# Attention of the first batch: when denominators, their inverses, the bias of v and the weight sums are done

## The chip, the cores and the metric

The kernel runs on one core of a Trainium2 chip. The metric is the device time of one execution in microseconds. The median of three runs of the kernel before is 2653.88 us (2652.91 to 2655.13).

## What is computed

Two layers on x of shape (4, 1024, 32, 32), everything in float32. Only the first one matters here; the second (three convolutions with batch norms and a residual) follows it and is not touched. Cut to what matters, for each of the four batches and N = 1024 tokens:

```python
x = hidden_states.reshape(B, C, N).transpose(0, 2, 1)
qkv = (x @ w_qkv.T + b_qkv).reshape(B, N, 3, nh, hd)      # 16 heads of 64
q, k = rmsnorm(rope(q)), rmsnorm(rope(k))
attn = softmax(einsum("bqhd,bkhd->bhqk", q, k) * hd ** -0.5)
ctx = einsum("bhqk,bkhd->bqhd", attn, v)
out = rmsnorm(ctx @ w_proj.T) + x
```

The kernel divides by the softmax's denominator after the product with v: the context of a head, summed over unnormalised exponentials, is multiplied by the inverse of the sum of the exponentials, and the bias of v is added at the end.

## The kernel before

**Stages.** The batches go one after the other through four projections (q, k, v, and the output projection after attention) and an attention. The projections are done by a fast matrix multiplication (Strassen's in Winograd's form, two levels), which needs sums of weight blocks. These sums are the same for every batch, so they are made once, during batch 0, and kept in DRAM (`wd`, `wd2`). A good part of them is made during batch 0's attention: 21 "parts" (the list `todo` in `program`, four from `prepare_blocks` and seventeen from `prepare`). A part loads four tiles of 128x512 through the SP queue into four buffers of a ring of eight (`chunk`), VectorE does four additions on them (lines 409 to 412 or 392 to 395), and the POOL queue writes the four results to DRAM (lines 414 or 397). At most two parts are loaded and waiting (`made`); `load_parts` fills up to two at score tile 3 of each unit.

**The attention's loop.** `attention` (line 767) handles one half of the queries (512 of 1024, `c` is 0 or 1), and in it eight pairs of heads (`hp`). One pair of heads in one half is called a unit here; batch 0 has sixteen, numbered 0 to 15. In a unit there are eight tiles of keys (`t`). For each, TensorE makes a score tile in PSUM (line 781, three buffers "sc", each of two banks), ScalarE its exponential (line 788) and VectorE adds it to the pair's running sum `d_` (lines 799 and 801). Then TensorE makes the contexts of the pair from the eight exponentials (line 810, one buffer "cx"), and ScalarE copies them out (lines 816, 819).

**Denominators.** Every second unit completes two pairs of heads. `late` holds their step: `sums_of_four` (line 856) sums the two `d_` over the partitions by eight matmuls with ones (line 863) into a buffer of the pool of the score tiles; `inverses` (line 905) copies that to SBUF by ScalarE (line 910) and sends it through DRAM, by the SP queue, into a tile of 128x16 (`to_few`, lines 898 and 902), on which the reciprocal is short (line 914); the result goes back to DRAM (line 915) and is spread over 64 partitions for each head (`spread`, line 932, two DMAs on SP). The step in `late` is taken at score tile 1 of the unit after the pair's; the reciprocal and what follows at that unit's end (`half_done`). At the end of the next odd unit `mean_of_v` (line 761) multiplies the contexts by the inverses on VectorE (line 764) and adds the bias of v on POOL (line 765). For the last two pairs `last_inverses` (line 920) is called at the end of the attention: reciprocal on a tile of 128x512 (line 924), DMAs by POOL, and the multiplication three products into the output projection (`means`). A buffer of scores named "skip" is taken before the last denominator.

**Order.** All engines but the queues work in the order in which the program is written (`manual_schedule`). In the projections a hand-written clock counts products: `after(n, step)` puts a step n products later, `product_done` advances the clock. The extra work in the attention (`extra`, the parts) is taken at the end of each unit, as many as a rounded share says (line 842). The batches 1 to 3 have no parts in their attention; in their first half (`fold`) they gather the sums of four pairs in two tiles T0 and T2 and treat them otherwise.

Of the kernel before, what the change touches and what calls it, by code (L numbers as in the profile page):

```python
# [11 lines left out]
F32 = mybir.dt.float32  # L12
AF = mybir.ActivationFunctionType
ALU = mybir.AluOpType
# [4 lines left out]
P = 128  # L19
# [4 lines left out]
NHP = C // (2 * HD)  # L24
CH = 512
NCH = N // CH
# [35 lines left out]
NH = NT // 2  # L62
# [23 lines left out]
def program(ctx, tc, x, wblk, w2, w3, vecs, cos, sin, out, bad):  # L86


    nc = tc.nc
# [26 lines left out]
    def col(name, i=0):  # L116
        return vec[:, COL[name] + i : COL[name] + i + 1]
# [40 lines left out]
    with tc.tile_pool(name=f"st{u}", bufs=2) as st, ExitStack() as s:  # L158

        tp = s.enter_context(tc.tile_pool(name=f"tp{u}", bufs=1))  # L160
# [24 lines left out]
        half = [slice(c * CH, (c + 1) * CH) for c in range(NCH)]  # L185
# [17 lines left out]
        def bank(kind, name):  # L203
            pool, shape = psum[kind]
            return pool.tile(shape, F32, tag=kind, name=name)
# [48 lines left out]
        def after(n, step):  # L254
            later.append((pace["at"] + n, step))
# [505 lines left out]
        def mean_of_v(q_all, c, hp, w, engine=nc.gpsimd):  # L761

            cx = q_all[:, hp, half[c]]
            nc.vector.tensor_tensor(cx, cx, w, ALU.mult)  # L764
            engine.tensor_scalar(cx, cx, col("bv", hp), None, ALU.add)  # L765

        def attention(b, c, q_all, k_all, v, probs_, late, ready, extra, slow, steps_in_all, load_parts, fold, then):


            at = half[c]  # L770
            sums_, contexts = [], []
            for hp in range(NHP):
                n = f"{b}_{c}_{hp}"
                rows = shifts(q_all, k_all, n, hp, c) if bad is None else None
                probs = []
                for t in range(N // P):
                    p = probs_[:, t]
                    sc = bank("sc", f"sc_{n}_{t}")
                    for keys in (low, high):
                        for j, d in enumerate((low, high)):  # L780
                            nc.tensor.matmul(  # L781
                                sc[keys, j], k_all[d, hp, t * P + keys.start : t * P + keys.stop], q_all[d, hp, at],
                                start=True, stop=bad is not None,
                            )
                    if bad is None:
                        for j in range(2):
                            nc.tensor.matmul(sc[:, j], ones[0:1, :], rows[j], start=False, stop=True)
                    nc.scalar.activation(p, sc, AF.Exp)  # L788
                    if t == 1:
                        if late:  # L790
                            late.pop(0)()
                        if fold and hp % 2 == 0:
                            d_ = fold[hp // 4][:, hp % 4 // 2 * 2 : hp % 4 // 2 * 2 + 2, :]
                        else:
                            d_ = acc.tile([P, 2, CH], F32, tag="tot", name=f"den_{n}")
                    if t == 3:
                        load_parts()
                    if t == 1:
                        nc.vector.tensor_tensor(d_, probs[0], p, ALU.add)  # L799
                    elif t > 1:  # L800
                        nc.vector.tensor_tensor(d_, d_, p, ALU.add)  # L801
                    probs.append(p)
                if (c, hp) == (NCH - 1, NHP - 1):
                    then()
                o = bank("cx", f"cx_{n}")
                for t in range(N // P):
                    for j in range(2):
                        h0 = (2 * hp + j) * HD
                        for i, keys in enumerate((low, high)):
                            nc.tensor.matmul(  # L810
                                o[j * HD : (j + 1) * HD, i], v[keys, t, h0 : h0 + HD], probs[t][keys, j],
                                start=(t == 0), stop=(t == N // P - 1),
                            )

                cx = q_all[:, hp, at]
                nc.scalar.copy(cx, o[:, 0])  # L816
                if b == 0 and (c, hp) != (NCH - 1, NHP - 1):
                    other = temp(f"cx_{n}")
                    nc.scalar.copy(other, o[:, 1])
                    nc.gpsimd.dma_start(cx, other, accum_op=ALU.add)  # L820
                else:
                    contexts.append((cx, o[:, 1]))
                sums_.append(d_)
                if hp % 2 == 1:
                    for r in ready:
                        mean_of_v(q_all, *r)
                    ready.clear()
                if fold:
                    halve(hp, d_, fold[hp // 4][:, hp % 4 // 2 * 2 : hp % 4 // 2 * 2 + 2, :])
                    if hp % 4 == 3:  # L830
                        eights.append((hp + 2, lambda n=n, hp=hp: sum_of_eight(b, n, hp, fold[hp // 4], ready)))
                if half_done and half_done[0][0] <= c * NHP + hp:
                    half_done.pop(0)[1]()
                if slow:
                    slow.pop(0)()

                if waiting:
                    next_waiting()
                slots = NCH * NHP - 1
                if extra and steps_in_all == 0 and hp > 0:  # L840
                    extra.pop(0)()
                for _ in range(len(extra) - -(-steps_in_all * max(slots - 1 - c * NHP - hp, 0) // slots) if steps_in_all else 0):
                    extra.pop(0)()
                if contexts:
                    nc.vector.tensor_tensor(contexts[0][0], *contexts.pop(0), ALU.add)
                if eights and eights[0][0] <= c * NHP + hp:
                    eights.pop(0)[1]()
                if hp % 2 == 0 or fold:
                    continue
                if (c, hp) == (NCH - 1, NHP - 1):  # L850
                    last_inverses(b, c, hp, n, sums_of_four(n, sums_), ready)
                else:
                    late.append(lambda n=n, hp=hp, ds=sums_: inverses(b, c, hp, n, sums_of_four(n, ds), ready))
                sums_ = []

        def sums_of_four(n, sums_):
            if n == f"0_{NCH - 1}_{NHP - 1}":
                bank("sc", f"skip_{n}")
            dn = bank("sc", f"dn_{n}")[:, 0]
            for i, d_ in enumerate(sums_):  # L860
                for j in range(2):
                    q = slice((2 * i + j) * QH, (2 * i + j + 1) * QH)
                    nc.tensor.matmul(dn[q, :], ones[:, :QH], d_[:, j], start=True, stop=True)  # L863
            return dn

        half_done, eights = [], []
        low, high = slice(0, P // 2), slice(P // 2, P)

        def halve(hp, d_, home):
# [35 lines left out]
        def inverses(b, c, hp, n, dn, ready):  # L905


            r = temp(f"rec_{n}")
            k = 2 * ((b * NCH + c) * NHP + hp - 1)
            nc.scalar.copy(r, dn)  # L910
            few, rows = to_few(n, k, 4, r[::QH, :])

            def invert():
                nc.vector.reciprocal(few, few)
                nc.sync.dma_start(rows, few)
                spread(c, hp, n, ready, [dens[k + j : k + j + 3 : 2, :] for j in range(2)])

            half_done.append((0, invert))

        def last_inverses(b, c, hp, n, dn, ready):  # L920
            k = 2 * ((b * NCH + c) * NHP + hp - 1)
            r = temp(f"rec_{n}")
            nc.scalar.copy(r, dn)
            nc.vector.reciprocal(r, r)
            nc.gpsimd.dma_start(dens[k : k + 4, :], r[::QH, :])
            spread(c, hp, n, ready, [dens[k + j : k + j + 3 : 2, :] for j in range(2)], nc.gpsimd)
# [263 lines left out]
        for b in range(B):  # L1190
# [29 lines left out]
            v = room  # L1220
# [30 lines left out]
            slow = [lambda: None] * 3 + [lambda f=f: add_residual(f) for f in range(NT)] if b > 0 else []  # L1251
            probs_ = xp.tile([P, N // P, 2, CH], F32, tag="x", name=f"p_{b}")
            fold = [None, None]
            if b > 0:

                fold[0] = [tp.tile([P, NH, CH], F32, tag=t, name=f"den_{b}_{t}") for t in ("T0", "T2")]
# [8 lines left out]
            for c in range(NCH):  # L1265
                if (b, c) == (B - 1, NCH - 1):
                    extra = filters()
                attention(
                    b, c, q_all, k_all, v, probs_, late, ready, extra, slow, steps_in_all, load_parts, fold[c], then
                )  # L1270
            psum_for("proj")
            room = v_room(f"to_{b}")
# [50 lines left out]
        w = conv1_weights("last")  # L1323
# [364 lines left out]
```

## Time and profile before

| | us |
|---|---|
| median of three runs | 2653.88 |
| profiled execution | 2659.62 |
| its span, first to last instruction | 2657.8 |
| TensorE matmul busy | 2628.8 (99%) |
| VectorE busy | 2142.4 (81%) |
| ScalarE busy | 1120.3 (42%) |
| POOL busy | 474.6 (18%) |
| batch 0's attention, first score tile to the projection's first product | 289.61 to 522.41 |
| batch 1's attention, the same | 868.62 to 1095.39 |

A busy TensorE is counted from overlapping matmuls, so the share of 99% hides waits that are shorter than the work around them; these are read from the starts of consecutive groups in the timeline. Lines of the timeline have the start, the duration, the engine, the line of the kernel, the operation, the tiles written and read, the shapes and the count; a bracket holds the idle time before it and what ended it. PEld is the loading of weights into TensorE, SPq and POOLq are queues that issue DMAs.

### The profile page before, as it was taken

The numbers are of one execution on the slowest core, as the hardware profiler recorded it, in microseconds if no ns is written. First come the engines' busy times: TensorE is split into PE (matmuls) and PEld (weight loads), VectorE is DVE, ScalarE is ACT, GpSimd is POOL, SyncE is SP. The second block draws the span as 40 slices with busy tenths as digits, with TensorE's granted clock in tenths as the row PEclk, the third lists the DMA queues.
The fourth block names the chain that finished last, engine by engine and source line by source line (L and its number), as shares of the span: only waits on it lengthen the run. The fifth ranks groups of instructions, "written<-read, shape, count | busy, mean of one in ns | idle before, by whom it ended". The sixth has DMA issues, their size and how long they took to land.

```text
span 2657.8 us, 40523 instructions
## 1 busy us (share of the span) xinstructions
PE 2628.8 (99%) x15434; PEld 1628.7 (61%) x15434; DVE 2142.4 (81%) x2595; ACT 1120.3 (42%) x1568; POOL 474.6 (18%) x592
## 2 busy tenths in 40 slices
PE   9999999999999999999999999999999999999997
PEld 4448533488888333688886333888884335846843
DVE  4577899997787877888888767987988779877987
ACT  2222465523342555433343555233425654312266
POOL 2542243401011221200111222000111221020000
PEclk9999999999999999999999999999999999999999
DMA  7897788777577452467776531666774443683165
GB/s 270 290 263 211 214 245 245 238 223 232 174 189 212 82 103 59 117 186 222 186 190 166 96 77 35 211 204 177 193 212 90 85 105 85 208 278 96 64 238 206
DMA packets 252794, 463.66 MB, mean 174 GB/s; under 512 B 32176, under 2 KB 124896, under 8 KB 252592
## 3 DMA queue, kind: packets, MB, share of 16 engines
q1 hardware_dynamic: 196672, 287.80, 35.2%
q0 software_dynamic: 47856, 156.40, 23.6%
q10 hardware_dynamic: 8064, 16.78, 1.8%
q8 instruction: 125, 2.05, 0.3%
q14 instruction: 77, 0.63, 0.1%
HBM read 329.53 MB, written 97.01 MB: 160 GB/s over the span
## 4 chain that ended last, share of the span: by engine, by line
PE 66%; DVE 1%; DMA 1%; ACT 0%; issue 0%; ACTq 0%
PE sc L781 13%; PE cx L810 12%; PE p_y L485 9%; PE p_v L480 8%; PE p_q L485 6%; PE p_k L485 6%; PE c L1592 4%; PE c2x L1453 2%; PE c L1015 2%; PE c2y L1453 2%; PE c L974 1%; PE c1s L1015 1%; PE dn L863 0%; DVE V L1388 0%; PE c1a L1015 0%; DMA cosT<-in_cos_dram 0%
## 5 line engine op out<-in xcount | busy, mean ns | idle before, releaser
L788 ACT ACTIVATE p<-sc 128x1024 f32<-128x1024 f32 x512 | 478.1, 1049 | 17.7 <-PE sc L781 17.4
L781 PE MATMUL sc<-q,k 64*64 64x512 f32 x4096 | 456.2, 591 | 0.0
L801 DVE TENSOR_TENSOR den<-den,p 128x1024 f32<-128x1024 f32 x312 | 385.2, 1235 | 37.2 <-ACT p L788 5.1
L810 PE MATMUL cx<-p,to 64*64 64x512 f32 x3072 | 338.3, 589 | 0.0
L781 PEld LDWEIGHTS sc<-q,k 64*64 64x64 f32 x4096 | 149.6, 132 | 293.7 <-ACT p L788 149.5
L810 PEld LDWEIGHTS cx<-p,to 64*64 64x64 f32 x3072 | 117.5, 133 | 212.1 <-issue 211.0
L480 PE MATMUL p_v<-w_v,x 128*128 128x256 f32 x928 | 210.1, 380 | 1.0 <-DVE x L451 1.0
L485 PE MATMUL p_y<-q,w_y 128*128 128x256 f32 x928 | 209.8, 380 | 0.7 <-issue 0.7
L485 PEld LDWEIGHTS p_y<-q,w_y 128*128 128x128 f32 x928 | 176.1, 190 | 27.7 <-issue 4.1
L480 PEld LDWEIGHTS p_v<-w_v,x 128*128 128x128 f32 x928 | 176.2, 190 | 26.1 <-DVE x L451 2.0
L816 ACT COPY q<-cx 128x512 f32<-128x512 f32 x64 | 37.5, 585 | 348.1 <-PE cx L810 348.1
L765 POOL TENSOR_SCALAR q<-q,vec 128x512 f32<-128x512 f32 x56 | 111.6, 2002 | 290.0 <-DVE q L764 290.0
L485 PE MATMUL p_q<-to,w_q 128*128 128x256 f32 x672 | 152.2, 380 | 0.0
L485 PE MATMUL p_k<-to,w_k 128*128 128x256 f32 x672 | 152.2, 380 | 0.0
L485 PEld LDWEIGHTS p_q<-to,w_q 128*128 128x128 f32 x672 | 127.7, 190 | 18.5 <-issue 1.2
L485 PEld LDWEIGHTS p_k<-to,w_k 128*128 128x128 f32 x672 | 127.6, 190 | 18.3 <-issue 1.2
L810 PE MATMUL cx<-p,rq 64*64 64x512 f32 x1024 | 112.8, 589 | 0.0
L1592 PE MATMUL c<-h,w 128*128 128x512 f32 x256 | 110.3, 593 | 0.5 <-ACT h L1495 0.5
L799 DVE TENSOR_TENSOR den<-p 128x1024 f32<-128x1024 f32 x52 | 63.5, 1222 | 42.8 <-ACT p L788 42.8
L801 DVE TENSOR_TENSOR den_T<-den_T,p 128x1024 f32<-128x1024 f32 x72 | 88.2, 1225 | 7.9 <-DVE den_T L801 0.5
L480 PE MATMUL p_v<-w_v,t 128*128 128x256 f32 x384 | 90.1, 379 | 1.2 <-DMA w_v<-wdf 1.2
L485 PE MATMUL p_y<-to,w_y 128*128 128x256 f32 x384 | 90.3, 380 | 0.2 <-DMA w_y<-wdf 0.2
(497 smaller groups left out, 4308.8 us busy)
## 6 DMA issues: line engine op xcount, KB each, us to landing
w_v<-wd2f SPq DMA_DIRECT2D x112, 256.0 KB, 2.9
w_y<-wd2f SPq DMA_DIRECT2D x112, 256.0 KB, 3.1
w_q<-wd2f SPq DMA_DIRECT2D x84, 256.0 KB, 3.0
w_k<-wd2f SPq DMA_DIRECT2D x84, 256.0 KB, 2.8
wd2f<-w_pre POOLq DMA_DIRECT2D x68, 256.0 KB, 4.5
q<-qs POOLq DMA_DIRECT2D x64, 256.0 KB, 5.5
k<-ks POOLq DMA_DIRECT2D x64, 256.0 KB, 4.5
x1df<-y POOLq DMA_DIRECT2D x32, 512.0 KB, 6.1
```

Of the source, the lines that this page charges most:

```text
L480: nc.tensor.matmul(o[:, q].rearrange("p (g f) -> p g f", g=2), r[:, i, q * P : (q + 1) * P], wt[:, :, i, :], skip_group_check=True, **at,)
L485: nc.tensor.matmul(o[:, q], wt[:, q, i, :], r[:, i, :], skip_group_check=True, **at)
L765: engine.tensor_scalar(cx, cx, col("bv", hp), None, ALU.add)
L781: nc.tensor.matmul(sc[keys, j], k_all[d, hp, t * P + keys.start : t * P + keys.stop], q_all[d, hp, at], start=True, stop=bad is not None,)
L788: nc.scalar.activation(p, sc, AF.Exp)
L799: nc.vector.tensor_tensor(d_, probs[0], p, ALU.add)
L801: nc.vector.tensor_tensor(d_, d_, p, ALU.add)
L810: nc.tensor.matmul(o[j * HD : (j + 1) * HD, i], v[keys, t, h0 : h0 + HD], probs[t][keys, j], start=(t == 0), stop=(t == N // P - 1),)
L816: nc.scalar.copy(cx, o[:, 0])
L1015: nc.tensor.matmul(o, wt[:, i, :], rows(i), start=first and i == 0, stop=last and i == NH - 1, skip_group_check=True,)
L1453: nc.tensor.matmul(o[:, r * TR * TC : (r + 1) * TR * TC], uw[2 * h + r, j][:, i * PL + f * P : i * PL + (f + 1) * P], vt[b, i][:, 2 * h + ...
L1592: nc.tensor.matmul(os[i], w3t[k][f // NH][:, f % NH, :], h2[b, k][:, half[c]], start=(k == 0), stop=(k == NPT - 1),)
```

## The change

In batch 0 alone (`b == 0`), except for the rounding of the parts, which only batch 0 has:

- The step in `late` (denominators of two pairs) is taken behind score tile 3 instead of tile 1. The running sums are kept in four slots of two tiles, T0 and T2 (`own`), instead of two buffers of the pool `acc`.
- The reciprocal, its DMA back and the spread (`half_done`) are put one unit later: at score tile 2 of the next odd unit, instead of the end of the unit of the denominators.
- At the end of an odd unit VectorE still multiplies by the inverses; the bias of v is now added by ScalarE (`mean_and_bias`, `biases`), behind the exponentials of tiles 5 and 6 of the next unit. In the last unit VectorE does both.
- The last denominators are put half a step of the clock (one block of eight matmul instructions) into the output projection, in a buffer of that stage's pool "o2"; "skip" goes.
- The number of weight parts taken at the end of each unit is rounded the other way. By unit they were 1, 1, 2, 1, 2, 1, 1, 2, 1, 2, 1, 1, 2, 1, 2 and are 2, 1, 2, 1, 1, 2, 1, 2, 1, 1, 2, 1, 2, 1, 1.

```diff
--- before.py
+++ after.py
@@ -764,7 +764,7 @@
             nc.vector.tensor_tensor(cx, cx, w, ALU.mult)
             engine.tensor_scalar(cx, cx, col("bv", hp), None, ALU.add)
 
-        def attention(b, c, q_all, k_all, v, probs_, late, ready, extra, slow, steps_in_all, load_parts, fold, then):
+        def attention(b, c, q_all, k_all, v, probs_, late, ready, extra, slow, steps_in_all, load_parts, fold, then, own):
 
 
             at = half[c]
@@ -786,10 +786,16 @@
                         for j in range(2):
                             nc.tensor.matmul(sc[:, j], ones[0:1, :], rows[j], start=False, stop=True)
                     nc.scalar.activation(p, sc, AF.Exp)
+                    if t == (3 if b == 0 else 1) and late:
+                        late.pop(0)()
+                    if t in (5, 6) and biases:
+                        biases.pop(0)()
+                    if b == 0 and t == 2 and half_done and half_done[0][0] <= c * NHP + hp:
+                        half_done.pop(0)[1]()
                     if t == 1:
-                        if late:
-                            late.pop(0)()
-                        if fold and hp % 2 == 0:
+                        if b == 0:
+                            d_ = own[hp % 4 // 2][:, hp % 2 * 2 : hp % 2 * 2 + 2, :]
+                        elif fold and hp % 2 == 0:
                             d_ = fold[hp // 4][:, hp % 4 // 2 * 2 : hp % 4 // 2 * 2 + 2, :]
                         else:
                             d_ = acc.tile([P, 2, CH], F32, tag="tot", name=f"den_{n}")
@@ -823,7 +829,12 @@
                 sums_.append(d_)
                 if hp % 2 == 1:
                     for r in ready:
-                        mean_of_v(q_all, *r)
+                        if b > 0:
+                            mean_of_v(q_all, *r)
+                        elif (c, hp) == (NCH - 1, NHP - 1):
+                            mean_of_v(q_all, *r, nc.vector)
+                        else:
+                            mean_and_bias(q_all, *r)
                     ready.clear()
                 if fold:
                     halve(hp, d_, fold[hp // 4][:, hp % 4 // 2 * 2 : hp % 4 // 2 * 2 + 2, :])
@@ -839,7 +850,7 @@
                 slots = NCH * NHP - 1
                 if extra and steps_in_all == 0 and hp > 0:
                     extra.pop(0)()
-                for _ in range(len(extra) - -(-steps_in_all * max(slots - 1 - c * NHP - hp, 0) // slots) if steps_in_all else 0):
+                for _ in range(len(extra) - steps_in_all * max(slots - 1 - c * NHP - hp, 0) // slots if steps_in_all else 0):
                     extra.pop(0)()
                 if contexts:
                     nc.vector.tensor_tensor(contexts[0][0], *contexts.pop(0), ALU.add)
@@ -848,22 +859,36 @@
                 if hp % 2 == 0 or fold:
                     continue
                 if (c, hp) == (NCH - 1, NHP - 1):
-                    last_inverses(b, c, hp, n, sums_of_four(n, sums_), ready)
+
+                    def last(ds=sums_):
+                        last_inverses(b, c, hp, n, sums_of_four(n, ds), ready)
+
+                    if b == 0:
+                        after(0.5, last)
+                    else:
+                        last()
                 else:
                     late.append(lambda n=n, hp=hp, ds=sums_: inverses(b, c, hp, n, sums_of_four(n, ds), ready))
                 sums_ = []
 
         def sums_of_four(n, sums_):
             if n == f"0_{NCH - 1}_{NHP - 1}":
-                bank("sc", f"skip_{n}")
-            dn = bank("sc", f"dn_{n}")[:, 0]
+                dn = bank("o2", f"dn_{n}")
+            else:
+                dn = bank("sc", f"dn_{n}")[:, 0]
             for i, d_ in enumerate(sums_):
                 for j in range(2):
                     q = slice((2 * i + j) * QH, (2 * i + j + 1) * QH)
                     nc.tensor.matmul(dn[q, :], ones[:, :QH], d_[:, j], start=True, stop=True)
             return dn
 
-        half_done, eights = [], []
+        half_done, eights, biases = [], [], []
+
+        def mean_and_bias(q_all, c, hp, w):
+            cx = q_all[:, hp, half[c]]
+            nc.vector.tensor_tensor(cx, cx, w, ALU.mult)
+            biases.append(lambda: nc.scalar.activation(cx, cx, AF.Identity, bias=col("bv", hp)))
+
         low, high = slice(0, P // 2), slice(P // 2, P)
 
         def halve(hp, d_, home):
@@ -915,7 +940,7 @@
                 nc.sync.dma_start(rows, few)
                 spread(c, hp, n, ready, [dens[k + j : k + j + 3 : 2, :] for j in range(2)])
 
-            half_done.append((0, invert))
+            half_done.append((c * NHP + hp + 2 if b == 0 else 0, invert))
 
         def last_inverses(b, c, hp, n, dn, ready):
             k = 2 * ((b * NCH + c) * NHP + hp - 1)
@@ -1251,6 +1276,9 @@
             slow = [lambda: None] * 3 + [lambda f=f: add_residual(f) for f in range(NT)] if b > 0 else []
             probs_ = xp.tile([P, N // P, 2, CH], F32, tag="x", name=f"p_{b}")
             fold = [None, None]
+            own = None
+            if b == 0:
+                own = [tp.tile([P, NH, CH], F32, tag=t, name=f"den_{b}_{t}") for t in ("T0", "T2")]
             if b > 0:
 
                 fold[0] = [tp.tile([P, NH, CH], F32, tag=t, name=f"den_{b}_{t}") for t in ("T0", "T2")]
@@ -1266,7 +1294,7 @@
                 if (b, c) == (B - 1, NCH - 1):
                     extra = filters()
                 attention(
-                    b, c, q_all, k_all, v, probs_, late, ready, extra, slow, steps_in_all, load_parts, fold[c], then
+                    b, c, q_all, k_all, v, probs_, late, ready, extra, slow, steps_in_all, load_parts, fold[c], then, own
                 )
             psum_for("proj")
             room = v_room(f"to_{b}")
```

## The prediction

> **What bounds the kernel now.** I read the stage table first, then TensorE's timeline, then VectorE's and the queues' in batch 0's attention, which is all that the change touches.
>
> ```profile
> core 0: us, PE busy (x) PEld busy (x) DVE busy (x) ACT busy (x) POOL busy (x), PEclk, DMA share, GB/s
> 283.00:526.00 243.00, 241.91 (x2160) 86.17 (x2160) 222.33 (x236) 142.62 (x172) 92.31 (x124) 1.00 0.78 236
> 857.00:1096.00 239.00, 239.00 (x2154) 88.55 (x2153) 184.10 (x176) 134.98 (x154) 52.44 (x47) 1.00 0.37 75
> ```
>
> TensorE (PE) bounds both stages. But batch 0 (first row) also has VectorE (DVE) at 222 of 243 us and the DMA engines at 0.78, where batch 1 (second row) has 184 of 239 and 0.37: in batch 0 VectorE is nearly a second bound.
>
> ```profile
> 374.52 1.90 PE L781 MATMUL sc<-q,k 64*64 64x512 f32 x16
> 376.35 1.91 PE L863 MATMUL dn<-den,ones 128*32 128x512 f32 x8
> 378.19 5.38 PE L781 MATMUL sc<-q,k 64*64 64x512 f32 x48
> ...
> 463.66 1.06 PE L863 MATMUL dn<-den,ones 128*32 128x512 f32 x8
> 464.65 5.38 PE L781 MATMUL sc<-q,k 64*64 64x512 f32 x48
> ...
> 519.21 1.05 PE L863 MATMUL dn<-den,ones 128*32 128x512 f32 x4
> 520.62 1.05 PE L863 MATMUL dn<-den,ones 128*32 128x512 f32 x4 [0.36 <-DVE den L801]
> 522.41 3.69 PE L485 MATMUL p_y<-q,w_y 128*128 128x256 f32 x16 [0.73 <-issue]
> ```
>
> The only loss is at the denominators. Undisturbed, one costs 0.99 us to the next start (463.66 to 464.65). In unit 6 (a unit is one pair of heads of one half, counted 0 to 15) it costs 1.84, in unit 10 1.56 (434.46 to 436.02), and the last takes 3.20 to the projection's first product. Lost: 0.85 + 0.57 + 2.2 = **3.62 us**. That is what the change can win. The last 0.73 is labelled "issue", but the product starts at 522.38, just after ScalarE's copy of that denominator ends at 522.31 (L923, 521.72 + 0.585): I take it as that wait.
>
> ```profile
> 318.87 0.69 DVE L409 TENSOR_TENSOR w_blk<-w_blk,w_blk 128x512 f32<-128x512 f32 x1
> ...
> 321.65 1.22 DVE L799 TENSOR_TENSOR den<-p 128x1024 f32<-128x1024 f32 x1
> 322.97 7.87 DVE L801 TENSOR_TENSOR den<-den,p 128x1024 f32<-128x1024 f32 x6
> 332.80 0.25 DVE L914 RECIPROCAL few<-few 128x16 f32<-128x16 f32 x1 [1.96 <-DMA few<-densf]
> ```
>
> VectorE's unit is read here: weight sums (four operations, 2.75 us a part), then seven additions (9.11 us to the next start), then the inverse, which waited 1.96 us for its round trip.
>
> ```profile
> L406 SPq DMA_DIRECT2D w_blk<-in_wblk_dram x5: 328/328/328, 318.5 to 327.0; - x5
> DMA to landing us min/median/max: 5.0/5.7/6.0
> ```
>
> The loads of the third weight part start at 318.5, when the first part's writes (issued by POOL from 310.09) have landed and its ring buffers are free; the fourth is issued at 320.4 and lands 6 us later, at **326.5**.
>
> ```profile
> 505.98 0.33 SPq L915 DMA_DIRECT2D densf<-few  x1
> 508.71 1.26 SPq L932 DMA_DIRECT2D inv<-densf  x2
> 511.75 2.08 SPq L383 DMA_DIRECT2D w_y<-in_wblk_dram  x2
> ```
>
> SP's queue runs in order: inverse back, its spread, then the projection's first weights.
>
> [...]beside POOL's bias (L765, 2.0 us each) two of four weight sums per pair take 0.98 to 1.06 us, not 0.69. [...]The 8 KB inverses land 1.4 to 5.2 us after issue: [...]the spread is load. [...]Around each 128*32 denominator among 64*64 tiles the neighbouring groups are some 0.16 us long; the change keeps their number.
>
> **The change, part by part.** TensorE's base: a unit is 13.74 us (6.87 scores + 6.87 contexts), one with a denominator 14.89.
>
> (1) *Denominator behind score tile 3 instead of 1.* It moves 2 x 0.86 us later, to unit start + 3.54; its second half, which needs the newer sum, to + 4.05. Both old stalls inside the stage go if the sum is there by then. The four `own` sums free VectorE of the two-buffer limit. ScalarE's copy moves along, and SP's two DMAs behind it.
>
> (2) *Weight parts sooner.* Parts popped per unit were 1,1,2,1,2,1,1,2,1,2,1,1,2,1,2; now 2,1,2,1,1,2,1,2,1,1,2,1,2,1,1. No work is added, but unit 0 now makes two. Follow VectorE from the first part, 306.98: + 2 x 2.75 + 9.11 = 321.6 for unit 1's sum. Unit 2 starts at 317.13, its denominator wants that sum at 321.2: **0.4 lost**. Next VectorE wants the third part, one unit sooner than before. It lands at 326.5 at the earliest I can argue from its buffers: VectorE idles 4.9 us. Then 326.5 + 2.75 + 9.11 (unit 2) + 2 x 2.75 + 9.36 (unit 3, inverse included) = 353.2. Unit 4 starts at 317.13 + 14.89 + 0.4 + 13.74 = 346.2 and wants the sum at 350.2: **3.0 lost**. Bounds: 0.2, if loads landed in 3.2 us; 4.2, if the second part's writes, now in the same stretch, delay them by 1.2.
>
> (3) *Inverses a unit later* (at tile 2 of the odd unit, behind the first addition). VectorE no longer waits for `few` (4.1 us in three waits). But the multiplication by the spread inverse (L764) keeps its place, so reciprocal, DMA back, spread of two DMAs must now fit beside six additions: 8.1 us. In the trace reciprocal to landed spread takes 8.4, 7.0, 6.9, 10.6, 11.1, 8.9 and 9.4 us: mean 8.9. This is the **added wait**: some 0.7 us per pair, at least 0, at most 3.0. Behind it on VectorE stand the weight sums, the next additions, hence the next denominator. A pair of units costs VectorE 2 x 9.11 + 0.25 + 2 x 0.6 + 3 x 2.75 = 27.9, with the wait 28.6, TensorE 13.74 + 14.89 = 28.6: even. After unit 4 the later sums stand some 2.5 us ahead of their denominators (units 6, 8, 10: for instance 380.3 against 382.8), so I book **0**. SP's loads behind the spread start some 3 us later in odd units; that meets the same slack.
>
> (4) *Bias of v by ScalarE.* Off POOL: 12 x 2.0 us; VectorE wins back 6 x 0.7 us (used above: undisturbed 2.75). On ScalarE: 12 x 0.72 us (the same form, L631, 719 ns), behind tiles 5 and 6. ScalarE is busy 143 of 243 us; exponentials 6 and 7 come at most 1.4 us later, and contexts want tile 6 only 5.2 us after scores end: 0. Without that cover it would be 8.6 us. The two biases of the last pair but one go to VectorE: 2 x 0.55 us, in (5).
>
> (5) *Last denominators in the projection.* They stand behind its first product (1.73 us), in a bank of its own pool; the 2.2 us go if unit 15's sum is ready. By the chain above it ends some 0.5 to 1 us before. But SP reaches the projection's first weights only behind the spread of unit 15, now some 6.5 us later in the unit: issued at about unit start + 9.3, needed at 13.74, and the row above landed 5.7 us after issue, with two parts' writes in the way instead of one: **0.3**, 0 to 1.5. In the projection VectorE does the reciprocal of 3.35 us and sums behind two more operations; the sum wanted by the tenth product was 3.2 us early (534.83 against 538.0) and is now about even: **0.3**, 0 to 1.5.
>
> Sum: -3.62 + 0.4 + 3.0 + 0 + 0.3 + 0.3 = **+0.4 us**. Against the profiled execution's 2659.62 us (span 2657.8) that is 2660.0; the median of the runs, 5.7 us lower, is shifted alike: 2653.88 + 0.4 = 2654.3. Everything after the projection is paced by TensorE's products and moves along.
>
> **Rivals.** *A, the forecast*: the gain is given back at unit 4; 2652.6 to 2656. *B, the gain stays*: the third part lands in some 3.2 us. For it: loads elsewhere take 2.8 us (w_y, minimum). Against: DMA share in this stretch is 0.8. -3.62 + 0.4 + 0.2 = -3.0: 2650.9. *C, slower: VectorE becomes the bound through the wait for the spread.* If it takes 10.8 us, as in two of seven, each pair waits 2.7 and falls 2.0 us behind; four such pairs after unit 4, less 0.8 in the pair with two parts, less the 2.5 ahead: 4.7 us on top of A, 2659.0. It decides from a mean of about 9.5 us on. For it: the reciprocal now stands behind the weight sums, whose writes are then in flight. Against: SP's queue is otherwise empty there. *D*: TensorE's wait at 651 us for `w_q` (2.13 us, and the next eight matmuls took 3.68 instead of 1.89) goes or doubles: 3.9 us either way; nothing in its surroundings changes.
>
> **Numbers.** A 0.48, B 0.27, C 0.21, D 0.04. The range reaches from B's end with all stalls gone and a run's spread of 1 us, 2649.5, to C's 2659.2; less than 2 in 10 is left out. A measurement here tells 0.2% (5.3 us) from no change. Under 2648.6: part of B and D, 0.04; over 2659.2: C's tail and D, 0.09; between, 0.87.
>
> **What would show it.** Right: in the profile after, the denominators of units 6 and 10 cost 1 us, that of unit 4 some 4, VectorE idle near 322 to 326 for a `w_blk` load; 128x512 bias rows on ACT. Wrong: unit 4 without a stall (B), or stalls in units 8 to 14 with VectorE idle for `inv` (C).

## The result and the profile after

The kernel after takes **2683.74 us** (median of five runs, 2680.84 to 2686.30), the kernel before 2653.88 (2652.91 to 2655.73) beside it: ratio 1.0113, 95% interval 1.0101 to 1.0124. It is 30 us slower where 0.4 us was forecast. The profiled execution took 2682.35 us with a span of 2680.5, 22.7 us more than that of before, which lay 5.7 us over the median of its own runs.

The stage of the change can be timed without that spread: from the first score tile of batch 0 to the last product of its projection. Before: 289.61 to 607.25, **317.64 us**. After: 287.90 to 632.55, **344.65 us**, so +27.0. The remaining difference of the spans comes from elsewhere: the stage starts 1.7 us sooner, and between the projection and batch 1's attention 2.7 us less is lost (the wait at 651 us was 2.13 us with slow matmuls behind it, and is 1.28 now).

The stage table of the kernel after, first the stage that the prediction showed, then two stretches in which the granted clock (third number from the end) fell:

```profile
283.00:526.00 243.00, 232.43 (x2032) 78.87 (x2034) 196.98 (x212) 143.88 (x175) 62.88 (x104) 0.99 0.74 219
...
415.30:422.10 6.80, 5.69 (x24) 1.47 (x28) 3.54 (x5) 1.69 (x3) 0.00 (x0) 0.50 0.43 128
541.60:551.80 10.20, 6.33 (x15) 3.82 (x12) 9.83 (x12) 0.58 (x1) 0.58 (x1) 0.50 0.21 54
```

TensorE is busy 232 us of 243 instead of 242, VectorE 197 instead of 222: VectorE has not more to do, it waits. TensorE's timeline of the kernel after (start, duration, line, tiles, count, idle time and what ended it):

```profile
348.70 1.05 PE L882 MATMUL dn<-den_T,ones 128*32 128x512 f32 x4
352.10 1.05 PE L882 MATMUL dn<-den_T,ones 128*32 128x512 f32 x4 [2.35 <-DVE den_T L807]
353.09 3.67 PE L781 MATMUL sc<-q,k 64*64 64x512 f32 x32
...
412.28 1.05 PE L882 MATMUL dn<-den_T,ones 128*32 128x512 f32 x4
416.41 1.92 PE L882 MATMUL dn<-den_T,ones 128*32 128x512 f32 x4 [3.08 <-DVE den_T L807]
418.26 5.54 PE L781 MATMUL sc<-q,k 64*64 64x512 f32 x32
...
536.56 2.00 PE L485 MATMUL p_y<-q,w_y 128*128 128x256 f32 x8
538.49 1.05 PE L882 MATMUL dn<-den_T,ones 128*32 128x512 f32 x4
541.41 1.82 PE L882 MATMUL dn<-den_T,ones 128*32 128x512 f32 x4 [1.87 <-DVE den_T L807]
547.09 3.78 PE L485 MATMUL p_y<-q,w_y 128*128 128x256 f32 x8 [3.87 <-DVE q L856]
```

Wherever TensorE loses time here, a denominator's second half waits for the newer of the two sums (`den_T`, VectorE); at the end the second product waits too, for VectorE's addition of the last contexts (L856). Against the undisturbed 14.89 us, the units 2, 4, ... 14 are longer by 0.98, 3.39, 2.92, 6.87, 0.97, 1.87 and 3.47 us: 20.5, where before lost 1.4 in them. From the start of unit 15 to the projection's end it is 109.84 us instead of 101.89: 7.95 more. 20.5 - 1.4 + 7.95 = 27.0, the whole difference. In unit 8 and at the end the granted clock fell to 0.50 around the wait. In unit 8 the second half of the denominators took 1.85 us to the next start instead of 0.99, and the group of 32 score matmuls behind it 5.37 us (418.26 to 423.63) instead of 3.48: 2.75 of the 6.87 us.

What VectorE waited for between 283 and 551 us (us in all, times, the longest), and its timeline around two of these waits:

```profile
DVE q L889 <- DMA inv<-densf: 21.6, 5, 6.5
DVE w_blk L409 <- DMA w_blk<-in_wblk_dram: 5.4, 1, 5.4
DVE q L889 <- PE sc L781: 4.0, 1, 4.0
```

```profile
325.39 0.69 DVE L409 TENSOR_TENSOR w_blk<-w_blk,w_blk 128x512 f32<-128x512 f32 x1 [5.36 <-DMA w_blk<-in_wblk_dram]
...
407.00 1.22 DVE L805 TENSOR_TENSOR den_T<-p 128x1024 f32<-128x1024 f32 x1
408.38 0.25 DVE L939 RECIPROCAL few<-few 128x16 f32<-128x16 f32 x1 [0.16 <-DMA few<-densf]
408.55 7.81 DVE L807 TENSOR_TENSOR den_T<-den_T,p 128x1024 f32<-128x1024 f32 x6
419.59 1.29 DVE L889 TENSOR_TENSOR q<-q,inv 128x512 f32<-128x512 f32 x2 [3.23 <-DMA inv<-densf]
```

The multiplication by the spread inverses (L889) is the wait. In six pairs it waited 6.47, 4.00, 3.23, 2.65, 4.25 and 4.95 us: 25.6 in all. (The 4.00 is labelled with a score tile; the spread landed at that moment.) From the reciprocal's end to the landed spread it took 14.2, 11.7, 10.8, 10.2, 11.9, 12.6 and 10.5 us in the seven pairs, mean **11.7**; take 7.75 us off for the six additions between and each of the six waits comes out within 0.2 us. The only other wait of size inside the attention is the third weight part at 325.39, as forecast. SP's queue between reciprocal and spread:

```profile
409.05 1.19 SPq L383 DMA_DIRECT2D w_pre<-in_wblk_dram  x2
410.35 0.49 SPq L940 DMA_DIRECT2D densf<-few  x1
410.93 1.88 SPq L383 DMA_DIRECT2D w_pre<-in_wblk_dram  x2
414.36 1.25 SPq L957 DMA_DIRECT2D inv<-densf  x2
```

SP isn't among the engines whose order is written out: two weight loads stand ahead of the inverses' way back and two more ahead of their spread, where the kernel before had the two next to each other.

### The profile page after: what moved, and what is told of

The parts are those of the page before. It is cut to its first block, busy times and chain, and to the rows that moved or that the text cites. A ratio compares the mean times of both kernels' runs of the same rounds, so it can differ in the third digit from the quotient of the medians.

```text
span 2680.5 us, 40507 instructions
## 1 busy us (share of the span) xinstructions
PE 2637.4 (98%) x15434; PEld 1633.3 (61%) x15434; DVE 2140.3 (80%) x2597; ACT 1129.2 (42%) x1580; POOL 447.3 (17%) x578
## 5 line engine op out<-in xcount | busy, mean ns | idle before, releaser
L807 DVE TENSOR_TENSOR den<-den,p 128x1024 f32<-128x1024 f32 x216 | 267.9, 1240 | 26.9 <-ACT p L788 5.1
L807 DVE TENSOR_TENSOR den_T<-den_T,p 128x1024 f32<-128x1024 f32 x168 | 205.7, 1224 | 17.1 <-ACT p L788 0.5
L765 POOL TENSOR_SCALAR q<-q,vec 128x512 f32<-128x512 f32 x42 | 83.5, 1999 | 278.2 <-DVE q L764 278.2
L727 POOL DMA_DIRECT2D k<-ks x64 | 58.1, 1099 | 182.7 <-ACT p L788 71.2
```

Source lines behind the costliest of these rows:

```text
L727: nc.gpsimd.dma_start(dst[i::2, f, :], other[1 - i :: 2, :], accum_op=ALU.add)
```

## The experiments

In the table the stage is the stretch timed above. "Waits" is VectorE's time waiting for `few` (the denominators' round trip) and for the spread between 283 and 551 us, from the profile. Ratios are to the kernel before on the same chip, with 95% intervals.

| kernel | median us | ratio | stage | waits few / spread |
|---|---|---|---|---|
| before | 2653.88 | 1 | 317.6 | 4.1 / 0.6 |
| after | 2683.74 | 1.0113 (1.0101 to 1.0124) | +27.0 | 1.4 / 25.8 |
| part 3 alone | 2682.56 | 1.0107 (1.0091 to 1.0124) | +29.7 | 0 / 32.3 |
| after, part 3 undone | 2672.91 | 1.0070 (1.0053 to 1.0087) | +21.5 | 18.6 / 0 |
| part 1 alone | 2671.39 | 1.0066 (1.0052 to 1.0079) | +16.0 | 19.3 / 1.5 |
| after, part 2 undone | 2681.85 | 1.0106 (1.0089 to 1.0123) | +28.9 | 0.9 / 34.0 |
| after, back and spread by POOL | 2681.98 | 1.0107 (1.0090 to 1.0124) | +24.6 | 1.0 / 25.1 |
| after, one part in even units | 2684.24 | 1.0113 (1.0097 to 1.0128) | +30.1 | 6.6 / 23.1 |
| after, multiplication behind the parts | 2659.71 | 1.0019 (1.0011 to 1.0026) | +3.7 | 0 / 7.7 |
| after, multiplication a unit later | 2658.76 | 1.0013 (1.0007 to 1.0020) | +2.2 | 0.3 / 1.8 |
| multiplication a unit later, part 2 undone | 2657.73 | 1.0013 (1.0007 to 1.0020) | +4.0 | 1.1 / 2.1 |
| multiplication a unit later, part 2 undone, last addition first | 2653.20 | 0.9997 (0.9989 to 1.0005) | -1.4 | 0.5 / 2.8 |
| multiplication a unit later, write by ScalarE's queue | 2664.37 | 1.0037 (1.0024 to 1.0049) | +8.7 | 0.4 / 1.2 |
| part 5 alone | 2658.40 | 1.0015 (1.0008 to 1.0021) | +4.6 | 3.3 / 1.5 |
| part 5 alone, last addition first | 2654.96 | 1.0001 (0.9992 to 1.0009) | -1.0 | 3.2 / 2.5 |

**Which part.** The first theory (S) was that the wait for the spread, which the change added, is the loss; the rivals were the weight parts (P), or that another wait takes its place when it is undone.

```diff
 (before, part 3 alone)
+                    if b == 0 and t == 2 and half_done and half_done[0][0] <= c * NHP + hp:
+                        half_done.pop(0)[1]()
...
-            half_done.append((0, invert))
+            half_done.append((c * NHP + hp + 2 if b == 0 else 0, invert))
```

> The kernel before with the inverses a unit later and nothing else. Theory S: 2666 us or more, with VectorE idle for inv in the even units. Theory P: 2652 to 2657 us.

Part 3 alone in the kernel before makes the whole loss: 2682.56 us, and VectorE waits in all seven pairs:

```profile
DVE q L764 <- DMA inv<-densf: 32.3, 7, 8.3
```

The same edit taken out of the kernel after (the two lines at tile 2 removed, the threshold 0 again):

> The changed kernel with the inverses back at the end of the unit of their denominators. Theory S (VectorE waits for the spread inverses, 25.6 us in six waits, because they now start seven to eight us before they are wanted): the waits for inv go, 2652 to 2660 us. Theory P (the third weight part, wanted one unit sooner, idles VectorE for 5.4 us in unit 2, and VectorE has no slack to make it up): it stays over 2674 us. A third outcome: the denominators now stand 1.7 us later, so the wait of VectorE for few, 4.1 us in the kernel before, grows to 10 us or more, and the time lies between, 2660 to 2670.

It gave back only about a third: 2672.91 us, 2.9 us above the range of the third outcome, whose mechanism it is. The wait for the spread is gone, and another has come up in its stead:

```profile
DVE few L937 <- DMA few<-densf: 18.6, 7, 4.9
DVE w_blk L409 <- DMA w_blk<-in_wblk_dram: 5.9, 1, 5.9
```

Now the reciprocal waits for the denominators' round trip in all seven pairs. In the kernel before `few` landed at 332.8, 358.1, 392.0, 422.6, 450.7, 477.0 and 505.2 us, and the reciprocals began at 332.8, 362.3, 392.0, 422.6, 451.4, 477.2 and 505.7: in six of seven pairs under 0.8 us of slack. Whether the denominators' place by itself has used that up, part 1 alone shows:

```diff
 (before, part 1 alone; "own" as in the change)
+                    if t == (3 if b == 0 else 1) and late:
+                        late.pop(0)()
                     if t == 1:
-                        if late:
-                            late.pop(0)()
```

> The kernel before with part 1 alone: four sums of their own, denominators behind score tile 3 instead of 1. Theory F (the round trip to few, which three of seven inverses waited for already, starts 1.7 us later in all seven, and VectorE, the second bound, pays for it): waits for few of 10 to 16 us instead of 4.1, 2659 to 2666 us. Rival N (VectorE has the slack, only the two stalls of units 6 and 10 go): 2652 to 2653.5 us with waits for few below 6 us.

```profile
DVE few L916 <- DMA few<-densf: 19.3, 6, 5.8
```

Theory F, and more strongly than it said: 2671.39 us, outside its 2659 to 2666, and 19.3 us of waits instead of 10 to 16. Part 1, which was to win 1.4 us, costs 16 us in the stage when it stands alone. The weight parts are not the cause; with the old rounding (`-(-steps_in_all * ... // slots)`) in the kernel after:

> The changed kernel with the old rounding of the weight parts. Theory S: the six waits for inv stay at 3 us or more each, the time stays over 2668 us, and only the idle time of unit 2 (5.4 us of VectorE) goes. Theory P: back to 2652 to 2660 us.

2681.85 us: P falls. (One of the six waits was 2.4 us, under the 3 us that S gave; the others were 4.5 to 9.2.)

**Is it the cover.** The wait should shrink by what the multiplication is moved back, whatever else the change holds. Two kernels move it, one by one or two weight parts, one by a unit:

```diff
 (after, multiplication behind the parts: the block is moved, in batch 0)
-                if hp % 2 == 1:
-                    for r in ready:
...
                     extra.pop(0)()
+                if hp % 2 == 1 and b == 0:
+                    for r in ready:
```

> The kernel after with one edit: at the end of an odd unit the multiplications by the spread inverses stand behind that unit's weight sums instead of ahead of them: 2.75 us more cover in units 3, 9, 11 and 13, 5.5 us in units 5 and 7. Theory W (wait = time to the landed spread less the cover, one for one): waits for inv of 3.7, 0, 0, 0, 1.5 and 2.2 us, 7.4 in all instead of 25.6, so about 18 us off: 2662 to 2668 us. Rival X (the weight sums, now earlier, put their writes and the next loads in front of the spread, which takes longer by as much): waits stay above 15 us and the time above 2673 us.

```diff
 (after, multiplication a unit later)
-                if hp % 2 == 1:
+                if hp % 2 == (1 if b > 0 or (c, hp) == (NCH - 1, NHP - 1) else 0):
                     for r in ready:
```

> The kernel after with one edit: the multiplications by the spread inverses (and with them the biases) stand at the end of the next even unit instead of the end of the odd unit, so that the spread has another 13.7 us of cover; only the pair of unit 15 keeps its place. Theory W (the whole loss is VectorE waiting for the spread, because the cover of 7.8 us is less than the 10 to 14 us from reciprocal to landed spread): the six waits of 25.6 us go, only the third weight part's 4.9 us stays, 2652 to 2659 us. Rival R (the other parts of the change cost as much by themselves, as the kernel with the inverses put back, 2672.9, suggests): above 2664 us although VectorE no longer waits for inv.

VectorE's waits, first behind the parts, then a unit later:

```profile
DVE q L891 <- DMA inv<-densf: 6.0, 3, 2.6
DVE w_blk L409 <- DMA w_blk<-in_wblk_dram: 5.4, 1, 5.4
...
DVE q L891 <- PE sc L781: 1.2, 1, 1.2
```

```profile
DVE w_blk L409 <- DMA w_blk<-in_wblk_dram: 5.2, 1, 5.2
...
DVE q L764 <- DMA inv<-densf: 1.8, 2, 1.5
DVE few L939 <- DMA few<-densf: 0.3, 1, 0.3
```

Behind the parts the multiplication waits 7.2 us (6.0 + 1.2) where 7.4 was worked out, so in the sum one for one; by pair it fits less well (2.6, 0, 0, 2.0, 1.4 and 1.2 us instead of 3.7, 0, 0, 0, 1.5 and 2.2). A unit later it doesn't wait at all before the projection (the 1.8 are in the last unit and the projection). The spread itself is no quicker: 11.7 and 11.9 us in the mean. The first run is below the range that W gave (2662 to 2668): taking the waits away takes the clock's falls away with them (from 283 to 551 us it is 1.00 in the mean in both kernels, 0.97 in the kernel after). In both kernels every unit from 6 to 14 is undisturbed (13.74 and 14.89 us); only units 2 and 4 keep 0.99 and 3.2 to 3.4 us, and the projection's start something. So the denominators at tile 3 (part 1), the bias by ScalarE (part 4) and the longer way of the inverses cost nothing in units 6 to 14 as soon as the multiplication is far enough behind. Rival R falls: what the kernel with part 3 undone lost was again part 1's wait on the same chain.

**Why the spread takes longer there.** In the kernel before the reciprocal's end to the landed spread was 8.6 us in the mean (the prediction's 8.9 counts from its start), 3.1 less than after. Of these 3.1 us 1.7 are the 8 KB write itself: from issue to landing it took 1.4 to 5.2 us before (mean 2.7) and 2.8 to 6.1 after (mean 4.3). Another 1.0 is the time until it is issued (up to 2.0 us, next to nothing before), and 0.4 the spread behind it (6.0 us before, 6.4 after). First idea: SP's order. The write and the spread of batch 0 on POOL's queue (`nc.gpsimd`):

> The changed kernel with the inverses written back and spread by the POOL queue, whose order is the program's, in batch 0. If theory S holds because SP's queue takes loads of weight parts before and between the two steps (two ahead, two or three between): reciprocal to landed spread falls from 12 us to 8 to 9.5, waits for inv to 1 us each, 2654 to 2664 us. If it holds because the DMA engines are full: the waits stay over 3 us, over 2672 us. Theory P: over 2674 us.

2681.98 us and 25.1 us of waits: no gain. The write took 3.3 to 7.1 us there, behind POOL's own weight writes, so SP's order didn't decide. Second idea: the number of weight parts in flight, with one part in even units and two in odd ones (`share = min(1 + hp % 2, len(extra))`):

> The kernel after with another sharing of the weight parts: one at the end of every even unit, two at the end of every odd one, so that ahead of every spread stand the writes and loads of one part, not of two as in units 3, 9, 11 and 13 of the kernel after. If those transfers lengthen the spread (two parts ahead: 12.2 us in the mean, one: 11.0), the spreads of these units take 1 to 1.5 us less and the waits for inv fall by 4 to 6 us in all: 2675 to 2680 us. Rival (what is in flight there makes no difference): waits of 24 us or more, 2682 us or more.

Rival by its time, 2684.24 us; the waits fell by 2.5 us to 23.1, less than the 4 to 6 forecast and more than the rival allowed. The spreads took 11.9, 10.7, 11.0, 10.6, 11.8 and 13.0 us in the first six pairs. The expectation miscounts one unit: in the kernel after, two parts stand ahead of the spread in units 3, 11 and 13 (14.2, 11.9 and 12.6 us), and one in unit 9. Of these three the first got shorter by 2.2 us, the others by 0.2 and not at all. Third, in the kernel with the multiplication a unit later, the write alone on ScalarE's queue behind tile 6 (`nc.scalar.dma_start(rows, few)`):

> The kernel with the multiplications a unit later (2658.8 us), and in it the inverses' 8 KB write goes out on ScalarE's queue, behind tile 6, where nothing else is queued in this stage; the spread stays on SP's queue. There the write landed 3.3 to 6.6 us after its issue (mean 4.7), in the kernel before 1.4 to 5.2 (mean 2.7). Theory Q (it stands behind the weight loads of its own queue): 1.4 to 2 us after its issue in all seven pairs. Rival E (the DMA engines are busy with the weights' loads and writes whatever queue it comes from): still 3.5 us or more in the mean. The time says little about either: 2656 to 2664 us.

Rival E: on a queue with nothing else in it the write landed 4.4, 4.3, 4.9, 4.1, 4.8, 5.5 and 3.3 us after its issue, mean 4.5 against 4.8 on SP. It isn't its own queue that holds it once it is issued. The time was 2664.37 us, ratio 1.0037 (1.0024 to 1.0049): in three units ScalarE stood 8.7, 4.8 and 4.4 us ahead of that write, the next exponential behind it; the trace puts that down to weight loads, and why isn't settled. What is different in the new place is how full the DMA engines are. The stretch from the reciprocal's end to the landed write, in the kernel before (DMA share and GB/s are the last two numbers):

```profile
333.10:334.50 1.40, 1.40 (x20) 0.41 (x16) 1.33 (x3) 1.40 (x3) 0.00 (x0) 1.00 0.07 6
...
392.20:393.70 1.50, 1.50 (x18) 0.46 (x13) 1.43 (x4) 1.50 (x3) 0.57 (x1) 1.00 0.32 52
422.90:427.10 4.20, 4.20 (x48) 1.42 (x44) 3.90 (x5) 4.20 (x6) 1.66 (x4) 1.00 0.89 241
451.70:456.90 5.20, 5.20 (x52) 1.69 (x48) 4.96 (x6) 5.05 (x6) 2.15 (x4) 1.00 1.00 280
```

and in the kernel after:

```profile
344.20:349.80 5.60, 5.56 (x48) 1.52 (x40) 5.18 (x6) 4.39 (x6) 1.32 (x2) 1.00 1.00 345
375.80:381.30 5.50, 5.50 (x52) 1.68 (x44) 5.08 (x5) 3.87 (x6) 1.28 (x2) 1.00 0.89 272
...
441.00:445.10 4.10, 4.10 (x40) 1.38 (x36) 3.79 (x4) 0.61 (x2) 0.00 (x0) 1.00 0.82 259
```

Before, the write met idle DMA engines in five of seven pairs (share 0.05 to 0.32, 1.4 to 2.7 us) and full ones in two (0.89 and 1.00: 4.2 and 5.2 us; their pairs took 10.4 and 10.8 us to the landed spread). After, it meets them full in all seven (0.82 to 1.01). The mean of 4.5 us on ScalarE's queue, against 4.8 on SP's, fits that. Two other traces bear on it. In the run with one part in even units the 21 parts have run out before the seventh pair. Its write went out at the new place and on SP's queue, met a DMA share of 0.06 and landed after 1.42 us; reciprocal to landed spread took 6.5 us instead of the 10.6 to 13.0 of the six pairs before it. In the kernel after with part 3 undone, where the way back starts at its old place, the write took 1.4 to 2.9 us (mean 1.9). So what makes the way long at the new place is, as far as these traces go, the weight parts' transfers. The share alone doesn't tell the time: the 2.9 us fell on a share of 0.06. A run with the transfers left out in all seven pairs wasn't tried.

**The last denominators.** Part 5 alone in the kernel before:

```diff
-                    last_inverses(b, c, hp, n, sums_of_four(n, sums_), ready)
+                    def last(ds=sums_):
+                        last_inverses(b, c, hp, n, sums_of_four(n, ds), ready)
+                    if b == 0:
+                        after(0.5, last)
...
-                bank("sc", f"skip_{n}")
-            dn = bank("sc", f"dn_{n}")[:, 0]
+                dn = bank("o2", f"dn_{n}")
```

> The kernel before with part 5 alone: the last denominators of batch 0 stand behind the first product of the projection, in a bank of the projection's pool, and the bias of the last pair but one is VectorE's. Theory G (in the kernel after it lost 7.5 us only because VectorE was late; here VectorE is in time): 1 to 2 us less than before, 2651.5 to 2653.5 us. Rival L (the denominators take one of the pool's buffers, so the second product comes to the bank of the last contexts one turn earlier and waits for their addition on VectorE whatever the rest does): 2655 to 2659 us, with TensorE idle between the denominators and the second product.

2658.40 us, rival L. TensorE and then VectorE at the end of its attention:

```profile
518.21 1.07 PE L874 MATMUL dn<-den,ones 128*32 128x512 f32 x8
523.28 3.75 PE L485 MATMUL p_y<-q,w_y 128*128 128x256 f32 x8 [4.00 <-issue]
526.82 4.71 PE L485 MATMUL p_y<-y,w_y 128*128 128x256 f32 x16
```

```profile
520.25 0.69 DVE L764 TENSOR_TENSOR q<-q,inv 128x512 f32<-128x512 f32 x1
520.97 0.49 DVE L765 TENSOR_SCALAR q<-q,vec 128x512 f32<-128x512 f32 x1
521.38 0.68 DVE L764 TENSOR_TENSOR q<-q,inv 128x512 f32<-128x512 f32 x1
522.10 0.49 DVE L765 TENSOR_SCALAR q<-q,vec 128x512 f32<-128x512 f32 x1
522.50 0.68 DVE L848 TENSOR_TENSOR q<-q,cx 128x512 f32<-128x512 f32 x1
```

The denominators are through in 1 us, and the second product then stands for 4.00 us. It starts at 523.28, just after the addition of the last contexts (L848) ends at 523.18: that addition reads the contexts' bank, and the second product is now the one that needs it (which bank it gets is read from the program's pools; that it waits for the addition the next run shows). On VectorE four operations on the pair before stand ahead of the addition, 2.25 us. The two groups behind the wait took 3.5 and 4.6 us to the next start, not 1.8 and 3.5 as in the next run: another 2.8 us at a low clock (granted from 283 to 551 us: 0.99 in the mean, 1.00 in the next run). With the addition put first in the last unit (`nc.vector.tensor_tensor(contexts[0][0], *contexts.pop(0), ALU.add)` ahead of `mean_of_v`):

> The kernel before with part 5 alone (as the earlier run of part 5, 2658.4), and at the end of unit 15 the addition of the last contexts ahead of the four operations on the last pair but one. If the second product waited only for that addition, which stood behind 2.3 us of VectorE's work, the wait of 4.0 us and the clock's fall behind it go: 2651 to 2653 us. Rival (the bank is not free sooner, or the sums behind are late): 2655 us or more.

```profile
520.57 1.97 PE L485 MATMUL p_y<-q,w_y 128*128 128x256 f32 x8 [1.68 <-issue]
```

The wait falls from 4.00 to 1.68 us, by the 2.3 us that stood ahead, and the clock stays up. That is only a little more than half of the wait: the addition still follows four sums for the projection, and the stage wins 1.0 us (2654.96 us, no difference that can be told).

**Part 2 and the whole.** In the kernel with the multiplication a unit later, the old rounding:

> The kernel after with two edits: multiplications at the end of the next even unit, and the old rounding of the weight parts. Against the run with the first edit alone (2658.8) it shows what the weight parts a unit sooner cost: by its profile 0.99 + 3.18 us at the denominators of units 2 and 4, so 2654 to 2655.5 us. Rival (VectorE then has the second part's work later, and the stalls come up in later units): 2657 us or more.

```profile
521.84 3.78 PE L485 MATMUL p_y<-q,w_y 128*128 128x256 f32 x8 [4.58 <-DVE q L856]
```

Rival, 2657.73 us: the stalls of units 2 and 4 go as expected, but the wait at the second product is 4.58 us instead of 1.35 in the kernel with the new rounding, because TensorE, without the two stalls, gets there 4.2 us sooner after the stage's start (231.2 instead of 235.3 us), and VectorE ends the addition only 1.0 us sooner (235.7 instead of 236.6): two parts stand at the end of unit 14 instead of one. Most of the early loss thus comes back as a wait for the last addition. In all, part 2 costs 4.2 us at its start and wins 6.0 at the end: 3.2 of waiting, and 2.7 in the two groups behind it, which ran at a low clock (granted from 283 to 551 us: 0.99 in the mean, 1.00 with the new rounding). With the addition first as well:

> The kernel after with three edits: multiplications by the inverses at the end of the next even unit, the old rounding of the weight parts, and at the end of unit 15 the addition of the last contexts ahead of the four operations on the last pair but one. If these three places are all that the change loses, no loss stays in the attention of batch 0 nor at its last denominators: the 3.6 us of before go, 2649.5 to 2651.5 us. Rival (a new place comes up, such as sums of the projection that come too late): 2653 us or more, and the profile names it.

At the rival's edge: 2653.20 us, ratio 0.9997 (0.9989 to 1.0005), stage -1.4. No unit loses anything; 1.14 us stay at the second product and 0.55 us at a later one (540.96). The change thus mended is as fast as the kernel before, and the best that was found; a gain isn't shown.

## Why the prediction was wrong

**Base.** The losses of before (0.85, 0.57 and 2.2 us) were read rightly: with the multiplication far enough behind, both stalls inside the stage are gone.

**(1) Right only beside other edits.** The denominators behind tile 3 remove those stalls, but SP's round trip that moves along ("behind it") ended on time by less than 0.8 us in six of seven pairs. That was in the trace and was not priced. Beside step (3) that wait doesn't arise (1.4 us in the kernel after), so it took the runs to show it.

**(2) Right.** 0.4 and 3.0 us were worked out for units 2 and 4 (the first from a start of unit 2 at 317.13; the profile has 317.24, so 0.3); 0.98 and 3.39 came, with VectorE idle 5.36 us for the third part (4.9 worked out). What was missed is the end: without these stalls, and with two parts instead of one at unit 14's end, TensorE waits that much longer for the last addition.

**(3) The step that failed.** The added wait was seen and placed, and its size was missed twice. First, "some 0.7 us per pair, at least 0, at most 3.0" took the spread's time from where it stood before (mean 8.9 us) against a cover of 8.1. In the new place it was 11.7 against 7.75 (both from the reciprocal's end): 25.6 us in six pairs. What was held against rival C, "SP's queue is otherwise empty there", was wrong: weight loads held the write back by 1.0 us in the mean. The larger part, 1.7 us in the mean, came with how busy the DMA engines are, 0.82 to 1.01 there and 0.05 to 0.32 in most pairs before; the prediction put the write's range of 1.4 to 5.2 us down to load ("the spread is load") and still took the mean. The two pairs of 10.4 and 10.8 us in the old profile were the two that met full engines, and were the sample to take. Second, "I book **0**": TensorE and VectorE had been found even at 28.6 us a pair, so 2.5 us of lead could cover less than one such wait. Rival C named this mechanism and a start at 9.5 us; it was given 0.21 and priced at 4.7 us.

**(4) Right.** The 12 biases take 8.6 us on ScalarE, 718 ns each (0.72 forecast). Undisturbed units from 6 to 14 in the mended kernels show that they are hidden. Part 4 wasn't run alone.

**(5) Wrong.** "The 2.2 us go if unit 15's sum is ready": the sum was ready in the run of part 5 alone, but the denominator's buffer in the pool "o2" brings the second product one turn earlier to the bank of the last contexts. That wait (4.00 us, and 2.8 at a low clock) wasn't in the list of waits. Of the two terms of 0.3 that were, neither showed in the kernel after. The one for the weights doesn't come out of its own figures: issued at 9.3 and landed 5.7 us later is 1.3 us behind 13.74. In the kernel after, SP issued the first weights at 522.34, ahead of the inverses' way back, so they were in time; with the old rounding (after, part 2 undone) it issued them at 531.80, and TensorE stood 3.39 us for them.

**The clock.** No step had it, though the kernel before shows it: behind the wait of 2.13 us at 651 us, which rival D names, the granted clock is 0.50 for 3.41 us. In the kernel after it is 0.50 for 6.83 us around a wait of 3.08 us, and for 10.24 us where 1.87 and 3.87 us follow each other. The three lengths are one, two and three times 3.41 us, and the two stretches in the kernel after start 126.29 us apart, 37 times 3.413 (at 415.27 and 541.56). A wait's length alone doesn't tell: the 2.13 us (before) were followed by 0.50, but 2.35 and 2.43 us (after, ending at 352.10 and 511.37) and 2.61 us (multiplication behind the parts, where the clock from 283 to 551 us is 1.00 in the mean) were not. What decides isn't shown.

## What to carry to other kernels

A chain that crosses several engines and DMAs between two fixed places has one slack; moving its start later (part 1) or one of its links later (part 3) draws on the same slack, and the wait comes up at the link that was not moved (19.3 us for `few` with part 1 alone, 32.3 us for the spread with part 3 alone). Take a moved transfer's time from the profile's moments in which the DMA engines are as full as at the new place, not from its mean (here 10.4 and 10.8 us, not 8.6; it took 11.7), and move its consumer along. When a bank is taken from another pool, ask which later product comes to which bank, and what still reads it (4.00 us with part 5 alone).

## What was not expected of the hardware

- An 8 KB write landed 1.4 us after its issue on idle DMA engines (kernel before, DMA share 0.05 to 0.32: 1.4 to 2.7), and 2.8 to 6.1 us on full ones (kernel after, 0.82 to 1.01); an otherwise empty queue hardly shortened it (write by ScalarE's queue: mean 4.5 us, against 4.8 on SP's).
- A wait of 4.00 us (part 5 alone) cost TensorE 6.8 us: the two product groups behind it took 8.1 instead of 5.3 us. Shorter waits did the same or not: 2.13 us (kernel before, at 651 us) was followed by half the clock for 3.41 us, 2.61 us (after, multiplication behind the parts) wasn't. A wait's length alone doesn't tell which, and what does isn't shown.
